# Reordering the head of a two-layer graph kernel: how many filter-spectrum steps stand between the head's rounds, and where a round's norm stands

## Chip, cores and metric

The kernel runs on one core of a Trainium2 chip. The metric is the device time of one execution in microseconds (us). The kernel before the change took 2195.82 us, the median of three runs between 2191.8 and 2198.84 us. The profile is of one execution, with a span of 2189.7 us.

## What is computed

The input is `x`, 128 graphs of 128 nodes with 256 features, and `adj`, one 128 x 128 adjacency matrix for each graph. Two layers follow each other, and each adds to `x` what it makes of the normalized `x`. Cut to what matters here:

```python
h = relu(layernorm(x))                                  # layer 0
xc = transpose(h)
c = relu(bn1(conv1d(xc, conv1_w)))                      # 1 tap
c = bn2(conv1d(c, conv2_w, pad=8))                      # 17 taps along the nodes
x_conv = transpose(relu(c + xc))
x_nmp = (exp(-dist(h)) * adj) @ relu(h @ w_msg.T + b_msg)
x = x + gru(concat(x_conv, x_nmp), h)
x = x + five_group_graph_conv(relu(layernorm(x)), adj)  # layer 1
```

All of it is in float32. The change is in the first fifth of the kernel: the norm, the one-tap convolution, and the preparation of the 17-tap convolution, which the kernel does in the frequency domain.

## The kernel before

The 128 graphs are worked on in blocks of four (`BB = 4`), 32 blocks in all. The first part of the kernel goes over them in two halves of 16 blocks (`HG = 64` graphs). For each half there is a head, which makes the spectra of the convolution's input, and a spectral stage, which multiplies them by the spectra of the filter taps, one frequency after the other. After both halves come the gates of layer 0 with layer 1 beside them; the change doesn't touch these.

**A head block** goes through five functions:

- `head_load` (line 189) brings 512 KB of `x` into a tile `ln`. There are three such buffers. The load goes through the SP queue, but for the very first.
- `head_norm` calls `layernorm`. For each of four graphs VectorE computes the statistics (lines 144 and 145), one instruction adds the epsilon (147), GpSimd raises it to the power -0.5 (149), and four VectorE instructions normalize in place (151). VectorE has to wait for GpSimd in between.
- `head_turn` transposes the block on TensorE (201) into two PSUM banks; ScalarE takes the relu into `ht` (202) and stores it for later, 512 KB through its own queue (203). From here the `ln` buffer is free for the load three blocks on.
- `head_conv1` is the one-tap convolution (215), again into two banks. VectorE adds the shift (218), and ScalarE takes the relu (219).
- `head_spectra` multiplies the result by a cosine and sine table (230) into four banks. VectorE copies two of them into the big tile `X` (236), ScalarE the other two (238).

**Tap spectra.** The spectra of the 17-tap filter are computed once, in eight tiles. `weight_spectra` is a generator: a tile takes four steps, and each step is 16 matmuls over four banks (172; a float32 matmul leaves two records in the profile, so a step is 32 records), which VectorE (178) and ScalarE (180) copy into a tile `sp` of 2560 KB, two banks each. There are two `sp` buffers. When a tile is complete it is stored into `vd` in DRAM through the SP queue (182), and the taps of the tile after the next are loaded, 1024 KB (162), also on the SP queue. The spectral stage reads `vd`, so it can't start before the last of these stores.

**How they are put together.** `some_spectra(k)` advances the generator by k steps. Six of the 32 steps are taken before the rounds of the first half; then `heads` runs one round for each block, and calls `between()` twice in a round. In the first half `between` is `some_spectra`, so two steps go with each round and the taps last for 13 rounds. In the second half `between` does nothing. Round i works on four blocks at once: the load of i + 3, the norm of i + 2, the transposition of i + 1, conv1 of i, and the spectra of i - 1. `heads_begin` fills this pipeline: it loads three blocks, normalizes two and turns the first; for the second half it is called two groups of frequencies before the end of the first spectral stage.

**What sets the order.** All PSUM tiles are handed out from one pool of eight banks in turn (`bank()`). The framework orders the instructions of each engine itself, when the kernel is built, and source order is the priority: something later in the source may move ahead of something earlier that is not ready by the framework's estimate. This can be seen in the profile, where the norm of one block is interleaved with the evictions of others on VectorE. Once built, that order is fixed.

Of the kernel before, what the change touches and what calls it, by code (L numbers as in the profile page):

```python
# [66 lines left out]
def gnn_kernel(ctx: ExitStack, tc: tile.TileContext, io, out: bass.AP):  # L67
# [16 lines left out]
    def bank():  # L84
        return psum.tile([P, 512], F32, tag="bank", name="bank")
# [21 lines left out]
    def constants():  # L107
        nc.sync.dma_start(vec, io["vec"])
        nc.sync.dma_start(wc1, io["wc1"].rearrange("(c p) o -> p c o", p=P))
        nc.sync.dma_start(fd, io["fd"])  # L110
        nc.sync.dma_start(idm, io["idm"])

        for j, v0 in enumerate((V_BN1, V_BN2)):
            g, b, m, v = (vec[:, v0 + 2 * q:v0 + 2 * q + 2] for q in range(4))
            sc, sh = bn[:, j, 0, :], bn[:, j, 1, :]
            ve = cst.tile([P, C], F32, name=f"bnve{j}")
            nc.vector.tensor_scalar(ve, v, EPS, None, op0=ALU.add)
            rs = cst.tile([P, C], F32, name=f"bnrs{j}")
            nc.gpsimd.tensor_tensor(rs, ve, mhalf[:, :C], op=ALU.pow)
            nc.vector.tensor_mul(sc, g, rs)  # L120
            nc.vector.tensor_mul(ve, m, sc)
            nc.vector.tensor_sub(sh, b, ve)

        bnb = hc.tile([P, 2 * C, P], F32, name="bnb")
        nc.vector.tensor_copy(bnb, bn[:, 0].rearrange("p q c -> p (q c)")[:, :, None].to_broadcast([P, 2 * C, P]))
        psb = bank()
        for q in range(2 * C):
            nc.tensor.matmul(psb[:, q * P:(q + 1) * P], bnb[:, q, :], ident, start=True, stop=True)
        nc.scalar.copy(bnr.rearrange("p q d -> p (q d)"), psb)
        nc.vector.tensor_mul(wc1, wc1, bnr[:, 0:1, :].to_broadcast([P, C, D]))  # L130
        nc.vector.tensor_add(brz, vec[:, V_IH:V_IH + 4], vec[:, V_HH:V_HH + 4])
# [28 lines left out]
    def taps_load(pool, c, q):  # L160
        w2 = pool.tile([P, WCH // 4, P], F32, tag="w2", name="w2", bufs=2)
        nc.sync.dma_start(w2, io["w2t"][:, c, q])
        return w2

    def weight_spectra(pool, c, q, w2):

        sp = pool.tile([P, LW, WCH], F32, tag="sp", name="sp", bufs=2)
        for t in range(WCH // 16):
            ps = [bank() for _ in range(4)]
            for j in range(4):  # L170
                for r in range(4):
                    nc.tensor.matmul(ps[r][:, j * LW:(j + 1) * LW], w2[32 * r:32 * r + KW, 4 * t + j, :],
                                     gt[32 * r:32 * r + KW, :], start=True, stop=True)
            for r in range(4):
                o0 = t * 16 + 4 * r
                dst, s = sp[:, :, o0:o0 + 4], ps[r][:, :4 * LW].rearrange("p (j d) -> p d j", j=4)
                if r % 2:
                    nc.vector.tensor_copy(dst, s)  # L178
                else:
                    nc.scalar.copy(dst, s)  # L180
            yield
        nc.sync.dma_start(vd[c, q], sp)
# [4 lines left out]
    def head_load(wk, i, queue):  # L187
        xs[i] = wk.tile([P, BB, D], F32, tag="ln", name="ln", bufs=3)
        queue.dma_start(xs[i], x[i * BB:(i + 1) * BB].rearrange("b n d -> n b d"))

    def head_norm(wk, i):
        layernorm(wk, xs[i], xs[i], P)

    def head_turn(wk, i):

        ln = xs.pop(i)
        ht = wk.tile([P, C, T], F32, tag="ht", name="ht", bufs=2)
        for c in range(C):
            ps = bank()
            for b in range(BB):  # L200
                nc.tensor.transpose(ps[:, b * N:(b + 1) * N], ln[:, b, c * P:(c + 1) * P], ident)
            nc.scalar.activation(ht[:, c, :], ps, AF.Relu)
        nc.scalar.dma_start(htd[i], ht)
        hcs[i] = ht

    def head_conv1(wk, i):
        ht = hcs.pop(i)
        h1 = wk.tile([P, BB, D], F32, tag="h1", name="h1", bufs=2)
        for h in range(BB // 2):
            ps = bank()  # L210
            pv = ps.rearrange("p (b d) -> p b d", b=2)
            for bb in range(2):
                b = 2 * h + bb
                for c in range(C):
                    nc.tensor.matmul(pv[:, bb, :], ht[:, c, b * N:(b + 1) * N], wc1[:, c, :],  # L215
                                     start=c == 0, stop=c == C - 1)
            hv = h1[:, 2 * h:2 * h + 2, :]
            nc.vector.tensor_tensor(hv, pv, sh1[:, None, :].to_broadcast([P, 2, D]), op=ALU.add)
            nc.scalar.activation(hv, hv, AF.Relu)
        h1s[i] = h1  # L220

    def head_spectra(X, i):
        h1 = h1s.pop(i)
        g0 = (i * BB) % HG
        for c in range(C):
            xv = X[:, c].rearrange("p a k (w g) -> p (a k) w g", w=2)
            for h in range(BB // 2):
                ps = bank()
                for bb in range(2):
                    nc.tensor.matmul(ps[:, bb * 2 * LW:(bb + 1) * 2 * LW], h1[:, 2 * h + bb, c * P:(c + 1) * P], fd,  # L230
                                     start=True, stop=True)
                s = ps[:, :4 * LW].rearrange("p (g w d) -> p d w g", g=2, w=2)
                dst = xv[:, :, :, g0 + 2 * h:g0 + 2 * h + 2]
                for w in range(2):
                    if h:
                        nc.vector.tensor_copy(dst[:, :, w], s[:, :, w])
                    else:
                        nc.scalar.copy(dst[:, :, w], s[:, :, w])
# [10 lines left out]
    def heads(wk, X, h, between):  # L249

        i0, i1 = h * NBH, (h + 1) * NBH
        for i in range(i0, i1 + 1):
            if i + 3 < i1:
                head_load(wk, i + 3, nc.sync)
            if i + 2 < i1:
                head_norm(wk, i + 2)
            if i + 1 < i1:
                head_turn(wk, i + 1)
            between()
            if i < i1:  # L260
                head_conv1(wk, i)
            between()
            if i > i0:
                head_spectra(X, i - 1)
# [60 lines left out]
    with front as es:  # L325
        xp = es.enter_context(tc.tile_pool(name="xp", bufs=1))
        hk = es.enter_context(tc.tile_pool(name="hk", bufs=1))
        X = xp.tile([P, C, NP_, 2, P], F32)
        with ExitStack() as ws:
            wp = ws.enter_context(tc.tile_pool(name="wp", bufs=1))  # L330
            todo = [(c, q) for c in range(C) for q in range(D // WCH)]
            head_load(hk, 0, nc.scalar)
            nc.sync.dma_start(gt, io["gt"])
            taps = [taps_load(wp, *todo[k]) for k in range(2)]
            head_norm(hk, 0)
            spectra = []

            def some_spectra(k=1):
                for _ in range(k):
                    if not spectra and todo:  # L340
                        spectra.append(weight_spectra(wp, *todo.pop(0), taps.pop(0)))
                    if spectra and next(spectra[0], STOP) is STOP:
                        spectra.pop(0)
                        if len(todo) > 1:
                            taps.append(taps_load(wp, *todo[1]))
                        some_spectra()

            some_spectra(3)
            constants()
            heads_begin(hk, 0)  # L350
            some_spectra(3)
            heads(hk, X, 0, some_spectra)
            while spectra or todo:
                some_spectra()
        bp = es.enter_context(tc.tile_pool(name="bp", bufs=1))
        nc.sync.dma_start(wms, io["wms"].rearrange("(c p) o -> p c o", p=P))
        nc.sync.dma_start(bms, row("bms", D + 3))
        nc.sync.dma_start(fw, row("fw", 5))
        nc.sync.dma_start(wih, io["wih"].rearrange("(c p) o -> p c o", p=P))
        nc.sync.dma_start(whh, io["whh"].rearrange("(c p) o -> p c o", p=P))  # L360
        for h in range(NH):
            if h:
                heads(hk, X, h, lambda: None)
            spectral(bp, X, h, lambda: heads_begin(hk, h + 1) if h + 1 < NH else None)
            if h == 0:
                gate_weights()

    wk = ctx.enter_context(tc.tile_pool(name="wk", bufs=1))
# [601 lines left out]
```

## Time and profile before

The profile's slices of time give each engine's busy time. The granted clock is a share of TensorE's full clock, and the DMA share is that of 16 DMA engines. Stages were told apart by the lines that run in them:

| stretch of the span | what runs | PE busy | DVE busy | clock | DMA share, GB/s |
|---|---|---|---|---|---|
| 20 to 40 us | head of half 0, first rounds | 17.84 of 20 | 13.47 | 0.66 | 0.85, 334 |
| 80 to 100 us | head of half 0, with tap spectra | 18.12 of 20 | 11.91 | 1.00 | 0.79, 289 |
| 120 to 140 us | the same | 18.15 of 20 | 11.93 | 0.83 | 0.76, 279 |
| 240 to 260 us | spectral stage of half 0 | 20.00 of 20 | 9.90 | 1.00 | 0.94, 312 |
| 380 to 400 us | head of half 1, no tap spectra | 20.00 of 20 | 16.34 | 1.00 | 0.45, 160 |

Over the whole span TensorE is busy for 2061.9 us (94%), VectorE for 1276.7 us (58%), ScalarE for 694.5 us and GpSimd for 580.5 us. PE is TensorE, DVE is VectorE, ACT is ScalarE, POOL is GpSimd, and SP is the engine that only issues DMAs. The first spectral matmul of half 0 starts at 205.91 us; that of half 1 at 431.56 us.

A busy time of TensorE has to be read with care: the ends of matmuls are modelled[...]. So the distance from the start of one group of matmuls to the next says more than the busy share.

### The profile page before, as it was taken

What the parts mean: (1) busy time and instruction counts of PE and PEld (TensorE: products, weight loads), DVE (VectorE), ACT (ScalarE), POOL (GpSimd) and SP (SyncE); (2) the same over time, 40 slices, a digit from 0 to 9 for tenths busy, and PEclk for the clock granted to TensorE, in tenths of its full rate; (3) what the DMA queues carried; (4) which work ended last, traced back from release to release, by engine and by line L of the source; (5) the groups of instructions that cost most, each with busy time, mean ns of one, the idle gap of its engine ahead of it and who ended that gap; (6) DMA issues with size and microseconds to landing.
All of it is one profiled execution on the core that took longest, in us unless ns stands there. A gap on an engine that the chain in (4) does not pass through costs nothing.

```text
span 2189.7 us, 31150 instructions
## 1 busy us (share of the span) xinstructions
PE 2061.9 (94%) x10981; PEld 1717.5 (78%) x10981; DVE 1276.7 (58%) x3518; ACT 694.5 (32%) x1424; POOL 580.5 (27%) x666
## 2 busy tenths in 40 slices
PE   7898988998999999999999999999999999999587
PEld 6777878987778778877888887788888778887576
DVE  6755447643555656665665666666566666655442
ACT  3442113411333333333333333333333333332222
POOL 3101531144222323322222332222233222212100
PEclk8998999999999999999999999999999999999787
DMA  8665984298412222221223222122322212221152
GB/s 335 252 242 184 300 273 172 94 298 256 143 52 73 70 62 72 72 71 52 71 87 109 83 71 72 51 72 88 110 83 72 71 51 71 92 81 53 55 151 84
DMA packets 200909, 260.11 MB, mean 119 GB/s; under 512 B 19378, under 2 KB 179378, under 8 KB 196146
## 3 DMA queue, kind: packets, MB, share of 16 engines
q1 hardware_dynamic: 192418, 219.85, 31.6%
q10 hardware_dynamic: 8336, 38.28, 4.7%
q8 instruction: 88, 1.44, 0.3%
q14 instruction: 67, 0.55, 0.1%
HBM read 175.63 MB, written 82.44 MB: 118 GB/s over the span
## 4 chain that ended last, share of the span: by engine, by line
PE 73%; DMA 8%; DVE 6%; POOL 3%; issue 1%; SPq 1%; ACT 0%; POOLq 0%; DVEq 0%; ACTq 0%
PE bank L550 29%; PE bank L299 5%; PE bank L586 5%; PE bank L773 5%; PE bank L790 5%; DMA hg<-xg 4%; PE bank L456 3%; PE bank L294 3%; PE bank L502 3%; PE bank L215 3%; PE bank L441 2%; PE bank L439 2%; PE bank L230 2%; DMA ln<-in_x_dram 1%; DMA w<-in_w_dram 1%; PE bank L617 1%
## 5 line engine op out<-in xcount | busy, mean ns | idle before, releaser
L550 PE MATMUL bank<-t,sw 128*128 128x256 f32 x1024 | 254.1, 381 | 1.1 <-DVE nn L565 1.1
L563 POOL TENSOR_TENSOR u<-u,m 128x256 f32<-128x256 f32 x96 | 73.1, 761 | 637.0 <-ACT m L561 613.0
L550 PEld LDWEIGHTS bank<-t,sw 128*128 128x128 f32 x1024 | 187.7, 191 | 24.6 <-DVE nn L565 1.2
L550 PE MATMUL bank<-t,wih 128*128 128x256 f32 x768 | 197.8, 380 | 0.0
L550 PEld LDWEIGHTS bank<-t,wih 128*128 128x128 f32 x768 | 146.2, 191 | 34.3 <-issue 10.7
L773 PE MATMUL bank<-ax,w 128*128 128x192 f32 (+12 forms) x592 | 129.4, 370 | 25.6 <-DMA w<-in_w_dram 22.7
L291 POOL TENSOR_TENSOR vs<-v 128x512 f32<-128x512 f32 x78 | 102.1, 1328 | 146.1 <-DMA v<-vd 81.1
L773 PEld LDWEIGHTS bank<-ax,w 128*128 128x128 f32 x592 | 104.4, 219 | 43.2 <-issue 29.7
L790 PE MATMUL bank<-w,hh 128*100 128x256 f32 (+8 forms) x552 | 133.3, 386 | 1.2 <-DMA w<-in_w_dram 1.2
L660 POOL TENSOR_TENSOR pw<-pw,mhalf 100x2 f32<-100x2 f32 (+7 forms) x69 | 50.3, 729 | 299.2 <-DVE pw L659 153.0
L456 PE MATMUL bank<-wms,ht 128*128 128x259 f32 x512 | 124.8, 387 | 5.1 <-DMA ht<-htd 5.1
L215 PE MATMUL bank<-wc,ht 128*128 128x256 f32 x512 | 127.2, 405 | 1.6 <-DVE sp L178 1.6
L586 PE MATMUL bank<-ht,whh 128*128 128x512 f32 x256 | 116.9, 600 | 0.0
L215 PEld LDWEIGHTS bank<-wc,ht 128*128 128x128 f32 x512 | 102.0, 205 | 17.4 <-DVE sp L178 1.8
L456 PEld LDWEIGHTS bank<-wms,ht 128*128 128x128 f32 x512 | 98.7, 193 | 20.8 <-issue 5.5
L550 PE MATMUL bank<-xc,wih 128*128 128x256 f32 x384 | 114.8, 381 | 0.0
L550 PE MATMUL bank<-xn,wih 128*128 128x256 f32 x384 | 114.7, 380 | 0.0
L790 PEld LDWEIGHTS bank<-w,hh 128*100 128x100 f32 (+8 forms) x552 | 92.2, 169 | 28.0 <-DMA w<-in_w_dram 1.4
L460 ACT ACTIVATE msg<-msg 128x512 f32<-128x512 f32 x64 | 40.3, 630 | 197.1 <-DVE msg L457 184.4
L289 DVE SCALAR_TENSOR_TENSOR s<-X 128x256 f32<-128x256 f32 x78 | 47.6, 613 | 94.2 <-PE bank L299 93.7
L149 POOL TENSOR_TENSOR rs<-ve,mhalf 128x4 f32<-128x4 f32 x32 | 32.3, 1008 | 232.9 <-DVE ve L147 232.9
L657 DVE BATCH_NORM_STATS2 st<-hg 100x6 f32<-100x256 f32 (+7 forms) x69 | 28.7, 419 | 108.8 <-DMA hg<-xg 108.7
(175 smaller groups left out, 4511.2 us busy)
## 6 DMA issues: line engine op xcount, KB each, us to landing
v<-vd SPq DMA_DIRECT2D x80, 512.0 KB
w<-in_w_dram SPq DMA_DIRECT2D x60, 512.0 KB
vd<-sp SPq DMA_DIRECT2D x8, 2560.0 KB
yd<-ys ACTq DMA_DIRECT2D x40, 512.0 KB
htd<-ht ACTq DMA_DIRECT2D x32, 512.0 KB
ht<-htd SPq DMA_DIRECT2D x32, 512.0 KB
ym<-yd SPq DMA_DIRECT2D x32, 512.0 KB
xt<-in_x_dram SPq DMA_DIRECT2D x32, 512.0 KB
```

The costliest lines, as they stand in the source:

```text
L215: nc.tensor.matmul(pv[:, bb, :], ht[:, c, b * N:(b + 1) * N], wc1[:, c, :], start=c == 0, stop=c == C - 1)
L291: nc.gpsimd.tensor_tensor(vs, vr, vi, op=ALU.add)
L294: nc.tensor.matmul(p1[:, :D], a[:, c], vs[:, c], start=c == 0, stop=c == C - 1)
L299: nc.tensor.matmul(ps[:, k * D:(k + 1) * D], u[:, c], w[:, c], start=c == 0, stop=c == C - 1)
L456: nc.tensor.matmul(ps[:, :D + 3], ht[:, c, b * N:(b + 1) * N], wms[:, c, :], start=c == 0, stop=c == C - 1)
L502: nc.tensor.matmul(ps[:, b * N:(b + 1) * N], msg[:, b, c * P:(c + 1) * P], e[:, b, :], start=True, stop=True)
L550: nc.tensor.matmul(ps, w, d, start=n == 0, stop=n == len(pairs) - 1)
L563: nc.gpsimd.tensor_tensor(got["u4"], got["u2"], got["m5"], op=ALU.add)
L586: nc.tensor.matmul(ps, whh[:, c, col:col + P], ht[:, c, :], start=c == 0, stop=c == C - 1)
L660: nc.gpsimd.tensor_tensor(pw[:n, 2:4], pw[:n, 0:2], mhalf[:n, 0:2], op=ALU.pow)
L773: nc.tensor.matmul(pv[:, q - q0, :], w1s[g][:, c, q * P:(q + 1) * P], ax[:, c, m0:m1], start=c == 0, stop=c == C - 1)
L790: nc.tensor.matmul(ps[:n, :D], hh[:, q, at:at + n], w2s[g][:, q, :], start=q == 0, stop=q == HID // P - 1)
```

## The change

The change has two parts, both in the head. Within a round of `heads`, conv1 of block i now comes first, then a call of `between`, then the transposition of block i + 1 and the norm of block i + 2, then the second `between`, then the spectra of block i - 1. Before, the norm came first, then the transposition, and conv1 stood between the two calls. This holds for both halves. And in the first half each `between` takes two steps of the tap spectra where it took one, so four steps go with a round, and the taps are through around block eight instead of around block thirteen.

It is meant to keep matmuls from standing behind a norm on VectorE's queue, and to have the taps' spectra stored early. No instruction is added or removed.

```diff
@@ heads @@
         for i in range(i0, i1 + 1):
             if i + 3 < i1:
                 head_load(wk, i + 3, nc.sync)
+            if i < i1:
+                head_conv1(wk, i)
+            between()
+            if i + 1 < i1:
+                head_turn(wk, i + 1)
             if i + 2 < i1:
                 head_norm(wk, i + 2)
-            if i + 1 < i1:
-                head_turn(wk, i + 1)
-            between()
-            if i < i1:
-                head_conv1(wk, i)
             between()
             if i > i0:
                 head_spectra(X, i - 1)
@@ with front as es @@
             heads_begin(hk, 0)
             some_spectra(3)
-            heads(hk, X, 0, some_spectra)
+            heads(hk, X, 0, lambda: some_spectra(2))
             while spectra or todo:
                 some_spectra()
```

## The prediction

> **What bounds the kernel now.** I read the 20 us slices first. From 206 us on nearly all of them have TensorE busy throughout at full clock; the change touches only the two heads (about 5 to 206 us and 320 to 432 us), so I asked for the stepped rounds of half 0 and for steady rounds of half 1 as two stretches. Columns: PE, PEld, DVE, ACT, POOL busy, clock, DMA share, GB/s.
> ```profile
> 28.85:179.00 150.15, 133.85 (x1305) 112.76 (x1306) 96.90 (x309) 56.81 (x149) 18.41 (x20) 0.92 0.67 246
> ...
> 345.00:410.00 65.00, 65.00 (x402) 60.87 (x401) 51.32 (x187) 28.38 (x77) 10.06 (x10) 1.00 0.43 155
> ```
> The reader should see that the half 1 rounds leave TensorE no gap, while the 13 stepped rounds of half 0 (150.15 / 13 = 11.55 us each) have 16 us of gaps, a clock of 0.92 and no engine that is full. The chain of waits in half 1 gives the undisturbed price of a round's pieces:
> ```profile
> 346.76 3.46 PE bank L215 x16
> 350.22 2.17 PE bank L230 x16
> 352.39 0.87 PE bank L201 x8
> ```
> So a plain round is 3.46 + 2.17 + 0.87 = 6.50 us of TensorE. A tap step is 1.06 us (32 records, from 94.34 to 95.40 us in the timeline). A stepped round before should take 6.50 + 2 x 1.06 = 8.62 us; it takes 11.55, a loss of 2.93 us a round. The timelines of TensorE, VectorE and SP around 160 us show how it is lost:
> ```profile
> 163.39 0.46 PE L172 MATMUL bank<-gt,w 17*128 17x80 f32 x6
> 166.83 1.96 PE L172 MATMUL bank<-gt,w 17*128 17x80 f32 x26 [2.98 <-DVE X L236]
> 168.72 6.10 PE L215 MATMUL bank<-wc,ht 128*128 128x256 f32 x16
> ```
> ```profile
> 165.47 0.76 DVE L144 BATCH_NORM_STATS2 st<-ln 128x6 f32<-128x256 f32 x2 [4.31 <-DMA ln<-in_x_dram]
> 166.14 0.54 DVE L236 COPY X<-bank 128x160 f32<-128x160 f32 x2
> ```
> ```profile
> 153.22 0.34 SPq L182 DMA_DIRECT2D vd<-sp  x1
> 153.66 10.20 SPq L189 DMA_DIRECT2D ln<-in_x_dram  x2
> ```
> Read backwards: conv1 ran at half clock (6.10 us for 16 records instead of 3.6). Ahead of it TensorE idled 2.98 us for a bank that VectorE's copies to X had to empty. They stood on VectorE behind the first statistics of a norm, which waited 4.31 us for its block of x. That block was issued at 153.66 us, just behind the 2560 KB store of a tap tile, and landed about 12 us later. In the stepped rounds VectorE waits so four times (10.0 us), and 13 times for GpSimd's power (14.3 us).
>
> [...] the busiest slice here, 180 to 200 us, has 354 GB/s at a share of 1.04[...].
>
> **The change part by part.**
>
> *Four steps a round.* Nothing is added: 26 steps stand in the rounds. They took 13 rounds at two; at four they take six rounds and a half. A four-step round needs 6.50 + 4 x 1.06 = 10.74 us of TensorE. VectorE, from the distances in its timeline: norm 3.0, wait for GpSimd 1.2, two shifts 1.2, eight tap copies at 0.41 = 3.3, four copies to X 1.0, in all 9.7 us. DMA: a tile's store and taps, a block of x and a block stored, by the page's sizes
> ```profile
> vd<-sp SPq DMA_DIRECT2D x8, 2560.0 KB
> ln<-in_x_dram SPq DMA_DIRECT2D x18, 512.0 KB
> ```
> are 2560 + 1024 + 512 + 512 KB = 4.72 MB[...]. If each round kept the loss of before, it would take 10.74 + 2.93 = 13.67 us[...]. [...] I take 14.2 us, with 13.2 and 16.5 as ends. The half round (two steps) takes 11.5. The other six of the old 13 rounds become plain, at 6.5 us as in half 1: 6 x 14.2 + 11.5 + 6 x 6.5 = 135.7 us against 150.15. **That is 14.5 us less.**
>
> *The stores are early.* They end near 125 us instead of 186.6, so the x loads of the last rounds and the first loads of vd no longer queue behind the last store. Before, the end of the head (191.1 to 205.9 us, 14.8 us for 3.46 + 2 x 2.17 = 7.8 us of TensorE) held VectorE waits for x of 2.8 and 0.5 us and TensorE idles of 3.0 and 0.8 us. Half 1's first norms still fall there; I count 3 us less. The spectral stage itself (PE busy 84.09 of 84.10 us) gains nothing.
>
> *conv1 first, the norm late (both halves).* The order adds no wait between instructions, but moves what stands behind a norm. Now the shifts of conv1 and the first tap copies have priority over it; behind it stand the second tap copies and the copies to X, hence spectra's banks. A norm takes 3.0 + 1.2 us on VectorE. Ahead of a blocked bank TensorE still has the transposition and two steps, 0.87 + 2.1 us, so up to 1.2 us a round may show, less than what a late block cost; it is inside the 2.93 us that I keep. In half 1 the start profits:
> ```profile
> 331.85 0.75 DVE L144 BATCH_NORM_STATS2 st<-ln 128x6 f32<-128x256 f32 x2 [6.43 <-DMA ln<-in_x_dram]
> ...
> 336.89 0.68 DVE L218 TENSOR_TENSOR h<-bank,bnr 128x512 f32<-128x512 f32 x1
> ```
> There a shift stands behind a norm that waits 6.43 us, and TensorE idles 6.43 us. With conv1 ahead, one more conv1 (3.5 us) can run in that wait; bounds 0 and 6, I take 3. The steady half 1 rounds are full on TensorE and stay at 6.5 us; VectorE there has only its 1.2 us wait for GpSimd to spare, so the new order could cost there: between 0 and 0.5 us in each of 13 rounds, I take 0.25, so 3 us, and another 1 us for the plain rounds of half 0.
>
> Sum: -14.5 - 3 - 3 + 3 + 1 = -16.5 us, so **2179 us**.
>
> **The rivals.**
>
> *DMA takes the place of the stalls, no change.* [...] For: [...] a store that waits for VectorE holds up the x loads behind it. Against: x loads have some two rounds until their norm. At 16.5 us a round: 99 + 11.5 + 39 = 149.5 us, a gain of 0.7 there; with 1 us from the end, 2194 us.
>
> *The new order stalls, slower.* A tile's first copy waits until the store two tiles back has landed, on VectorE and ScalarE ahead of all other evictions; before, a tile lasted 22.5 us and a store about 10, now they come within one round. If that wait and the cold clock after it bring the round to 18 us (108 + 11.5 + 39 = 158.5, +8.4), and half 1 pays 0.5 us in 13 rounds (+6.5) with 3 us back elsewhere, the time is 2207 us. For: a 2.98 us idle already cost a half clock.
>
> *All waits vanish.* Rounds [...] (79.2 + 10 + 39 = 128.2, -22), the end 6 and half 1's start 6 us shorter, no cost: 2162 us. For: each of these waits began at a late block. [...]
>
> **How the numbers follow.** Forecast 0.48, no change 0.19, slower 0.19, all waits vanish 0.14. The range reaches from the last case to near the slower one, 2160 to 2205 us. Faster by over 0.3% (below 2189.2 us) holds for the last case and nearly all of the first, and a little of the second: 0.64. Within 0.3%: 0.16. Slower (above 2202.4): 0.20.
>
> **What would show it right or wrong.** Right: seven rounds with tap matmuls of about 14 us, then plain ones near 6.5; the last vd store near 125 us; DMA share above 0.85 until then; the first spectral matmul near 190 us instead of 205.9; the head of half 1 no longer than before. Wrong: taps' copies that wait for a DMA, statistics that wait for x with evictions behind them as often as before, a granted clock below 0.9 up to 130 us, or half 1 rounds above 7 us.

## The result, and the profile after

The changed kernel takes 2182.4 us (median; 2179.8 to 2186.4), the one before 2195.9 us (2191.8 to 2198.8) beside it: a ratio of 0.9941, 95% interval 0.9919 to 0.9964, or 13.5 us less. The forecast was 2179 us. The time was met; the way to it was not, as the stages show. Executions of one and the same kernel differ by more than the change is worth (43 of the kernel before lie between 2186.3 and 2203.3 us), and each stage time below is from one profiled execution.

First the stages, in the view that gives busy time by stretch (columns: stretch, its length, busy time of PE, PEld, DVE, ACT and POOL with instructions, clock granted to TensorE, DMA share, GB/s): six four-step rounds; the plain rounds and the end of half 0; the head of half 1.

```profile
22.53:115.25 92.72, 81.61 (x994) 71.56 (x994) 60.20 (x168) 35.68 (x94) 16.99 (x18) 0.81 0.87 334
124.99:194.57 69.58, 64.98 (x368) 57.43 (x369) 51.25 (x181) 28.27 (x74) 13.17 (x12) 0.95 0.61 212
306.16:420.12 113.96, 106.49 (x634) 97.35 (x632) 75.32 (x251) 49.80 (x126) 14.60 (x14) 0.97 0.43 152
```

A four-step round takes 92.72 / 6 = 15.45 us, not 14.2. Its TensorE work is 10.74 us by the prediction's sum. TensorE is idle 92.72 - 81.61 = 11.1 us, 1.85 a round. The rest, (81.61 - 6 x 10.74) / 6 = 2.86 us, is time in which it works at half speed: the granted clock was 0.81, which the prediction had named as a sign against itself. So the loss of a round rose from 2.93 to 4.71 us.

One round in the timeline of TensorE (start, duration, engine and line; in brackets the idle before and who ended it):

```profile
84.58 3.62 PE L215 MATMUL bank<-wc,ht 128*128 128x256 f32 x16
88.13 2.03 PE L172 MATMUL bank<-gt,w 17*128 17x80 f32 x64
90.08 1.09 PE L201 MATMUL bank<-ident,ln 128*128 128x128 f32 x8
91.11 1.13 PE L172 MATMUL bank<-gt,w 17*128 17x80 f32 x32
92.60 1.52 PE L172 MATMUL bank<-gt,w 17*128 17x80 f32 x32 [0.37 <-DVE sp L178]
...
96.33 3.57 PE L230 MATMUL bank<-fd,h 128*128 128x160 f32 x12 [1.46 <-DVE sp L178]
99.69 4.57 PE L215 MATMUL bank<-wc,ht 128*128 128x256 f32 x16
```

The second bank of the spectra comes late, by 1.46 us, and then 12 records take 3.57 us (at full clock 12/16 of 2.17 us, so 1.63) and conv1 4.57 us instead of 3.46 (granted clock 0.50 over the 6.82 us from 94.78 us). But by the clock record, the trace's list of stretches at full and at half clock, this half clock began at 94.78 us, 0.1 us before that wait, so the late bank isn't what brought it. The 3.41 us ahead of it hold an idle of 0.37 us among tap steps (the columns of the stages again):

```profile
91.37:94.78 3.41, 3.04 (x68) 2.56 (x64) 2.19 (x11) 2.05 (x6) 1.01 (x1) 1.00 0.90 323
94.78:101.60 6.82, 5.36 (x18) 4.89 (x18) 3.80 (x12) 0.99 (x4) 0.00 (x0) 0.50 1.07 438
```

All six rounds have a half-clock phase. In four it began during the wait for that bank, in this one just before it, and in the first, which has no such wait, at 33.34 us behind idles of 0.16 us at most. On VectorE one sees what held the bank, here the same place of the round at 58 us:

```profile
61.62 0.76 DVE L144 BATCH_NORM_STATS2 st<-ln 128x6 f32<-128x256 f32 x2 [1.01 <-DMA ln<-in_x_dram]
...
64.71 0.74 DVE L151 TENSOR_SCALAR ln<-ln,mv,rs 128x256 f32<-128x256 f32 x2 [1.13 <-POOL rs L149]
65.36 0.88 DVE L178 COPY sp<-bank 128x320 f32<-128x320 f32 x2
```

The tap copies of the second pair of steps stand behind the norm and both its waits. In the waits of 20 to 190 us (in total, times, longest) the bank behind the norm is thus new, while the waits for x are shorter and more frequent than the four of before (10.0 us):

```profile
DVE st L144 <- DMA ln<-in_x_dram: 11.7, 10, 4.0
PE bank L230 <- DVE sp L178: 9.4, 5, 2.5
```

In half 1 one line answers to the one shown of before:

```profile
318.67 0.75 DVE L144 BATCH_NORM_STATS2 st<-ln 128x6 f32<-128x256 f32 x2 [8.16 <-DMA ln<-in_x_dram]
```

and TensorE still waits 6.41 us, until 324.95 us, for the relu of a transposed block that comes behind it. The head of half 1 takes 113.96 us, against 111.36 us before.

The difference can be added up from the starts of matmuls. "Start" is the first conv1, "rounds" from there to the conv1 of block 13, "end" from there to the first spectral matmul (us):

| kernel | start | rounds | end | first spectral matmul |
|---|---|---|---|---|
| before | 28.85 | 150.1 | 26.9 | 205.9 |
| after | 22.53 | 150.4 | 21.7 | 194.6 |
| new order, two steps | 22.3 | 156.4 | 21.1 | 199.8 |
| old order, four steps | 32.0 | 150.0 | 21.1 | 203.1 |

The last two rows are the first pair of experiments below, which split the change. A second profile of the changed half 0, from the run with tap-like matmuls in half 1, has 22.4, 153.4, 21.6 and 197.5 us: start and end repeat, the rounds only within 3 us.

The head of half 0 thus gains 6.3 us at its start and 5.2 us at its end, and nothing in the thirteen rounds. The cuts aren't quite even. A transposition and a tap step stood ahead of the first conv1 before and now come later, the step in the rounds and a transposition in the end. At full clock these are 0.87 + 1.06 = 1.93 us, so of the 6.3 us about 4.4 are saved (waits of 2.1 us, and half clock: 0.50 was granted from 22 to 28.85 us), the rounds gain 0.9 us and the end 6.1.

Of the rest, spectral stage 0 takes 111.6 instead of 114.3 us (-2.7), the head of half 1 +2.6, everything behind it +1.0; together -10.4 us of profile span (2179.3 against 2189.7). The -2.7 us are the tail of the old end: before, the stage began at half clock, and 5.21 us of it at 0.50 cost 2.6: from start to start 12 records took 5.24 us there, and behind it, at a clock of 1.00, 4 took 0.86 us, so that 12 would take 2.58.

```profile
205.91:211.12 5.21, 5.21 (x12) 4.13 (x13) 1.02 (x4) 0.57 (x1) 0.00 (x0) 0.50 0.00 0
```

### The profile page after: what moved, and what is told of

It is laid out like the page before. It is cut to its first block, busy times and chain, and to the rows that moved or that the text cites. A ratio compares the mean times of both kernels' runs of the same rounds, so it can differ in the third digit from the quotient of the medians.

```text
span 2179.3 us, 31120 instructions
## 1 busy us (share of the span) xinstructions
PE 2058.2 (94%) x10981; PEld 1716.7 (79%) x10981; DVE 1276.1 (59%) x3518; ACT 697.3 (32%) x1424; POOL 581.3 (27%) x666
## 4 chain that ended last, share of the span: by engine, by line
PE 75%; DMA 10%; DVE 8%; POOL 4%; issue 1%; SPq 1%; ACT 1%; POOLq 0%; DVEq 0%; ACTq 0%
PE bank L550 28%; PE bank L299 5%; PE bank L586 5%; PE bank L773 5%; PE bank L790 5%; PE bank L215 5%; DMA hg<-xg 4%; PE bank L456 4%; PE bank L230 3%; PE bank L294 3%; PE bank L502 3%; PE bank L441 2%; PE bank L439 2%; DMA ln<-in_x_dram 2%; PE bank L617 1%; DMA w<-in_w_dram 1%
## 5 line engine op out<-in xcount | busy, mean ns | idle before, releaser
L773 PE MATMUL bank<-ax,w 128*128 128x192 f32 (+12 forms) x592 | 131.2, 375 | 25.0 <-DMA w<-in_w_dram 22.4
L230 PE MATMUL bank<-fd,h 128*128 128x160 f32 x512 | 84.3, 321 | 10.4 <-DVE sp L178 9.4
```

What stands on the lines that cost most here:

```text
L773: nc.tensor.matmul(pv[:, q - q0, :], w1s[g][:, c, q * P:(q + 1) * P], ax[:, c, m0:m1], start=c == 0, stop=c == C - 1)
```

## The experiments

Three explanations of the 15.45 us stood first, by the names that the expectations use. DMA FLOOR: the rounds carry 0.87 of the DMA's share and can't be much shorter. BANKS: the late bank behind the norm costs its idle and lets the clock fall. BUFFERS: x comes late because there are only three buffers for it.

**New order, two steps a round.**

```diff
-            heads(hk, X, 0, lambda: some_spectra(2))
+            heads(hk, X, 0, some_spectra)
```

> The new order of a round, with the old two steps a round. Theory PACKING (the gain is that six stepped rounds become plain, the order by itself is worth little): 13 rounds of about 11.5 us as before, total 2191 to 2199 us. Theory ORDER (the gain is that conv1's evictions no longer stand behind a norm): rounds below 11 us, total about 2184 us.

Measured: 2194.7 us, ratio 0.9985 (0.9972 to 0.9997). The first spectral matmul comes 6.1 us earlier than before, but the head of half 1 takes 3.1 us longer (114.4 us), and spectral stage 0, which here waits 2.72 us just behind its first matmuls, 0.5 us.

**Old order, four steps a round.** This is the kernel before with one line changed, so the norm comes first, as it did.

```diff
-            heads(hk, X, 0, some_spectra)
+            heads(hk, X, 0, lambda: some_spectra(2))
```

> Four steps a round, with the old order (norm, transposition, steps, conv1, steps, spectra). Theory PACKING: most of the gain is here, first spectral matmul at 193 to 198 us, total 2182 to 2187 us. Theory ORDER: four steps behind a norm that comes first stall more than two did; no gain, 2195 us or more.

Measured: 2189.6 us, ratio 0.9977 (0.9965 to 0.9989); first spectral matmul 2.8 us earlier. Neither part alone gives the 0.9941. The order brings the early start (its first conv1 goes ahead of a transposition and a step that took 1.97 and 2.40 us before, at a granted clock of 0.50), and at two steps a round it pays for that with 6.3 us in the rounds. Four steps leave the rounds as they were, and the head of half 1 too (111.9 us). Either alone shortens the end by nearly 6 us, so this gain counts only once.

**Tap copies off VectorE.** All tap copies of the tile's first two steps go to ScalarE.

```diff
-                if r % 2:
+                if r % 2 and t >= 2:
```

> The changed kernel, with the tap copies of the two steps behind the norm all on ScalarE (VectorE keeps its half of the other two steps). Theory BANKS (four-step rounds take 15.4 us because spectra's second bank is emptied by a VectorE tap copy that stands behind the norm): that TensorE wait (five times 1.4 to 2.5 us) goes, rounds fall to 13.3 to 14 us, total about 2173 us. Theory DMA FLOOR (the rounds are set by 4.72 MB a round): rounds stay above 15 us, total within 3 us of the changed kernel, 2180 to 2185 us.

Measured: 2180.3 us, ratio 0.9938 (0.9915 to 0.9960): no better than the change. The wait at the spectra's bank is gone. In its place stand others (waits, 22 to 112 us):

```profile
DVE st L144 <- DMA ln<-in_x_dram: 19.1, 5, 7.0
PE bank L172 <- DVE sp L178: 8.3, 2, 6.1
ACT sp L180 <- DMA vd<-sp: 6.3, 2, 3.6
```

and the six rounds take 15.1 us on average, from 10.8 to 20.1. One of them (12.7 us) has no idle of TensorE that the timeline shows, so 15.4 is no floor; but it too has 3.4 us of half clock by the clock record. Another has neither. It takes 10.83 us, TensorE's own sum, at a clock of 1.00 and a DMA share of 0.94:

```profile
51.19:62.02 10.83, 10.82 (x170) 9.76 (x169) 7.01 (x21) 6.58 (x19) 1.74 (x3) 1.00 0.94 342
```

A single round is thus held neither by the DMA nor by its tap steps. The round behind it waits 6.13 us for a tap copy and takes 20.1.

**Loads of x on ScalarE's queue.**

```diff
-                head_load(wk, i + 3, nc.sync)
+                head_load(wk, i + 3, nc.scalar)
```

> The changed kernel, with the rounds' loads of x on ScalarE's DMA queue instead of SP's. Theory QUEUE (the blocks of x land late because they are issued and drained behind tap stores and vd loads): plain rounds of half 0 lose less than the 9 us they lose now, the 6.4 us wait at the start of half 1 shrinks, total 2172 to 2178 us. Theory BANDWIDTH (they are late because the DMA engines are full): no change, 2180 to 2185 us.

Measured: 2234.8 us, ratio 1.0179 (1.0153 to 1.0205), which no theory had. The issue of the load now has its place in ScalarE's own order, among copies and activations, as the stores of `ht` have in the changed kernel: there a relu ended at 61.41 us, the issue took 61.45 to 61.78 us, and the next tap copy began at 61.88 us. And x comes later than ever: VectorE's statistics wait 61.6 us in eight times, a four-step round takes some 24 us. That the loads wait behind ScalarE's work is the author's reading; the run's views don't show their issues. The run says nothing on the disputed cause, but something on queues: the loads did not come earlier on the queue that carries only the 512 KB of `ht` a round.

**A quarter of the store.** Only a quarter of each tap tile is stored, and the spectral stage reads that quarter again and again; three quarters of the tap spectra are left out. Once alone, once together with the tap copies on ScalarE.

```diff
-        nc.sync.dma_start(vd[c, q], sp)
+        nc.sync.dma_start(vd[c, q], sp[:, :LW // 4, :])
```

> The changed kernel, storing only a quarter of each tap tile (the first 20 of 80 columns) and reading that quarter again for every frequency; what is left out is three quarters of the tap spectra. A four-step round then moves 2.75 MB instead of 4.72. Theory DMA FLOOR: rounds fall from 15.4 to below 13.5 us, and granted clock over rounds rises. Theory BANKS (the stall at spectra's second bank, 1.4 to 2.5 us with a cold clock behind it, sets the round): rounds stay within 0.7 us of 15.4.

> The kernel with the tap copies behind the norm on ScalarE, also storing only a quarter of each tap tile (three quarters of the tap spectra are left out). If both DMA and banks bind, each alone hides the other: rounds of 11 to 12 us here, near TensorE's 10.7, where the copies alone gave 15.1. If DMA alone binds: the same as the quarter store by itself. If neither does: still about 15 us.

Measured: 2188.9 and 2198.6 us, one time each; four-step rounds of 12.3 to 22.6 and 15.4 to 19.7 us. For the first, 22 to 112 us:

```profile
22.00:112.00 90.00, 79.27 (x844) 70.08 (x841) 53.03 (x150) 30.49 (x79) 16.34 (x18) 0.74 0.55 185
```

The DMA share falls from 0.87 to 0.55, and the rounds get no shorter: DMA FLOOR, as the cause of 15.45 us, falls. But the runs don't isolate the rest. With the store shorter, VectorE's instructions come out in another order, the norm ahead of conv1's shifts, and so

```profile
92.18 0.75 DVE L144 BATCH_NORM_STATS2 st<-ln 128x6 f32<-128x256 f32 x2 [5.17 <-DMA ln<-in_x_dram]
```

holds the shift, hence a bank for 3.22 us; the clock (0.74) falls within that idle. The plain rounds behind are another matter: six of them take 42.0 and 41.8 us here, against 47.9 and 50.8 in the two profiles of the changed half 0.

**Three steps a round** (two, then one).

```diff
-            heads(hk, X, 0, lambda: some_spectra(2))
+            turn = [0]
+
+            def three():
+                turn[0] += 1
+                some_spectra(1 + turn[0] % 2)
+
+            heads(hk, X, 0, three)
```

> The new order with three steps a round (two in the first place, one in the second), so taps last 8.7 rounds and a round moves 3.8 MB [...] beside 9.7 us of TensorE. Theory DMA FLOOR: rounds of about 12.5 us; 8.7 of them and 4.3 plain ones against 6.5 and 6.5 are 8 us less than in the changed kernel, total about 2174 us. Theory BANKS: the loss a round stays near 4.7 us, rounds of 14.4 us; 8 us more than in the changed kernel, about 2190 us.

Measured: 2191.1 us, ratio 0.9977 (0.9963 to 0.9991). Rounds between 9.9 and 23.0 us; the first spectral matmul at 205.0 us.

**A fourth buffer for x** (room made by putting two start-up tensors into a tile that is free then).

```diff
-        xs[i] = wk.tile([P, BB, D], F32, tag="ln", name="ln", bufs=3)
+        xs[i] = wk.tile([P, BB, D], F32, tag="ln", name="ln", bufs=4)
```

> The changed kernel with four buffers for x instead of three (three small constants moved to make room), so a load no longer waits for a transposition. Theory BUFFERS (blocks of x land late in the first plain rounds and at the start of half 1 because their buffer comes free late): plain rounds of half 0 lose 2 to 4 us instead of 9, the 6.4 us wait at the start of half 1 goes, total 2168 to 2174 us. Theory BANDWIDTH (they are late because DMA is full): unchanged within 3 us, 2179 to 2186 us.

Measured: 2187.9 us, ratio 0.9968 (0.9947 to 0.9989). In the four-step rounds VectorE's statistics still wait four times for x, 5.7 us in all against 6.3, the bank stall of 1.46 us stays, and the rounds take 15.0 to 19.0 us. The six plain rounds take 47.1 us instead of 47.9, and half 1's start still waits 6.12 us. BUFFERS falls.

With these out of the way the half clock itself was in question. A half-clock phase occurred in nearly every four-step round, even in that round of the third experiment with 12.7 us and no visible idle. Hence a new theory, CLOCK: tap steps and transpositions, 5.1 us in one stretch, are themselves what lets the clock fall. The round of 10.83 us already speaks against it, and two runs tell it from BANKS.

**The stretch cut in two.** The spectra go between the first two steps and the transposition.

```diff
             between()
+            if i > i0:
+                head_spectra(X, i - 1)
             if i + 1 < i1:
                 head_turn(wk, i + 1)
             if i + 2 < i1:
                 head_norm(wk, i + 2)
             between()
-            if i > i0:
-                head_spectra(X, i - 1)
```

> The changed kernel with the pieces of a round in another order: conv1, two tap steps, the spectra of the block behind, the transposition of the next, the norm, two tap steps. Nothing is computed otherwise. CLOCK (the tap steps and the transposition, 5.1 us in one stretch, are themselves what lets the clock fall; spectra and the next conv1 then run at half clock): the stretches are now 2.1 and about 3.0 us with full matmuls between, so the granted clock of the four-step rounds rises from 0.81 to above 0.92, rounds fall from 15.4 to about 13.3 us, the first spectral matmul comes near 183 us, time about 2170 us. BANKS (an idle of 1.4 to 2.5 us of TensorE for a bank behind the norm is what lets it fall): the idle moves to another piece and the clock stays near 0.81, rounds 15 us or more, time 2180 to 2185 us. DMA [...]: rounds no shorter than 14.5 us, time 2175 us or more.

Measured: 2201.3 us, ratio 1.0033 (1.0017 to 1.0049), slower than before; granted clock 0.81 over 22 to 115 us, unchanged. The spectra run at full clock now, and the next conv1 takes the half clock, behind even a short idle:

```profile
90.84 2.44 PE L230 MATMUL bank<-fd,h 128*128 128x160 f32 x16
...
96.09 1.13 PE L172 MATMUL bank<-gt,w 17*128 17x80 f32 x30 [0.67 <-DVE X L236]
97.15 5.41 PE L215 MATMUL bank<-wc,ht 128*128 128x256 f32 x16
```

CLOCK's forecast is missed in each of its numbers.

**Tap-like matmuls in half 1.** Matmuls whose results nobody reads are added where half 0 has its steps: 32 of 17 rows per place in the first eight rounds, 16 of 128 rows in the later ones.

```diff
+        def fill():
+            k = 32 if calls[0] < 16 else 16
+            calls[0] += 1
+            ps = [bank() for _ in range(4)]
+            for m in range(k):
+                r, c, j = m % 4, m % 2, m // 4 % 4
+                rows = slice(32 * r, 32 * r + KW) if k == 32 else slice(0, P)
+                nc.tensor.matmul(ps[r][:, j * LW:(j + 1) * LW], wc1[rows, c, :P], gt[rows, :],
+                                 start=True, stop=True)
...
-                heads(hk, X, h, lambda: None)
+                heads(hk, X, h, fill)
```

> The changed kernel with matmuls added to the head of half 1, whose steady rounds (6.5 us, clock 1.0) have no tap steps, no copies of them and no store: into the two places of a round where half 0 has its steps, 32 matmuls of 17 rows each in the form of the tap steps (first eight rounds), or 16 matmuls of 128 rows each (the later rounds), about 2.1 us in either form; their results are read by nobody. CLOCK: without a stall and without DMA load the rounds with 17 rows lose their clock as half 0 does, granted clock about 0.8, 13 us a round instead of 10.7; the rounds with 128 rows stay at clock 1.0 and 10.7 us. BANKS or DMA: there is neither a late bank nor a load, so both kinds keep a clock of 1.0 and take 10.7 us. Kernel time 2182 plus 65 us (BANKS) or plus 80 to 85 us (CLOCK).

Measured: 2297.0 us, one time. Neither theory has it right, and that is the find. Rounds with 17-row matmuls alternate; here one with, one without a half clock, and one with 128 rows (stretches by busy time):

```profile
350.45:367.25 16.80, 15.84 (x171) 14.47 (x170) 7.94 (x30) 3.56 (x9) 2.01 (x2) 0.71 0.22 80
395.20:405.97 10.77, 10.77 (x171) 9.75 (x169) 3.54 (x10) 3.18 (x8) 0.00 (x0) 1.00 0.23 75
436.30:449.91 13.61, 13.61 (x106) 13.20 (x105) 5.78 (x20) 3.34 (x9) 1.01 (x1) 1.00 0.23 78
```

The same matmuls take 10.77 us without an idle, at clock 1.00, and 16.80 us where a bank comes 0.96 us late:

```profile
354.00 0.46 PE L370 MATMUL bank<-gt,wc 17*128 17x80 f32 x6
355.41 1.98 PE L370 MATMUL bank<-gt,wc 17*128 17x80 f32 x58 [0.96 <-DVE X L236]
357.32 1.92 PE L201 MATMUL bank<-ident,ln 128*128 128x128 f32 x8
359.17 3.72 PE L370 MATMUL bank<-gt,wc 17*128 17x80 f32 x64
```

The DMA share is 0.22 and 0.23, so the load of the DMA engines doesn't decide it. Against CLOCK: 17-row steps and transpositions without an idle kept the clock. (The 128-row matmuls take 3.69 us a place, not the 2.1 that the expectation assumed; their rounds of 13.61 us have TensorE full.) Against the forecast of BANKS: there was a late bank after all. In its mechanism BANKS stands here, in a sharper form: among tap steps an idle of 0.75 to 0.99 us (three of three: 0.96, 0.99 and 0.75 us) is followed by 10.2 us of half clock by the clock record, and the round is about 6 us longer, of which the idle itself is one. Rounds of 128 rows had no idle, so whether the same idle would cost the clock among full-row matmuls isn't tried. How short an idle suffices stays open as well: in the third experiment's round without a visible idle the second pair of steps took 2.57 instead of 2.03 us, so half a microsecond was lost in gaps too short for the timeline, and the clock fell. Nor does every such idle cost the clock. In the kernel before, one of 1.05 us within a transposition, with 0.56 us more among the tap step behind it, left it at 1.00, and so did idles of 0.97 us at 46 us and 1.05 us at 152 us:

```profile
81.41:88.24 6.83, 5.06 (x53) 4.01 (x52) 3.99 (x12) 3.56 (x11) 1.01 (x1) 1.00 0.81 335
```

A two-step round has one tap step (32 records, from 84.36 us here) between the transposition and conv1's matmuls of 128 rows, where the other has two steps in a row. Whether that is the reason isn't tested.

**Both edits at once**, tap copies on ScalarE and four buffers for x; and the same with x loaded four ahead, for half 1's start. (With four buffers the line numbers are 2 higher: L146 is L144.)

```diff
-                if r % 2:
+                if r % 2 and t >= 2:
...
-        xs[i] = wk.tile([P, BB, D], F32, tag="ln", name="ln", bufs=3)
+        xs[i] = wk.tile([P, BB, D], F32, tag="ln", name="ln", bufs=4)
```

> The changed kernel with two earlier single edits at once: the tap copies of the two steps ahead of spectra all on ScalarE, and a fourth buffer for blocks of x. Each alone took one of two idles away and gained nothing. IDLE (a short idle of TensorE, 0.5 us or more, among tap steps lets the clock fall [...]; without any idle the clock stays, as in the steady rounds with 17-row matmuls): with no late bank and no late x most rounds have no idle, granted clock of the four-step rounds above 0.9, rounds 13 to 13.5 us [...], first spectral matmul near 183 us, time about 2170 us. DMA or another wait in series (each idle that is taken away makes room for the next: copies on ScalarE that wait for a store): rounds 15 us or more, clock near 0.82, time 2178 to 2186 us.

and for the second of the pair, on top of that,

```diff
-        for k in range(1 if h == 0 else 0, 3):
+        for k in range(1 if h == 0 else 0, 4):
...
-            if i + 3 < i1:
-                head_load(wk, i + 3, nc.sync)
+            if i + 4 < i1:
+                head_load(wk, i + 4, nc.sync)
```

> The kernel of the run beside it, with blocks of x loaded four ahead instead of three, in both halves, so that the fourth buffer is used as soon as it is free. Half 0: as the run beside it, or a little later, since one more block of x goes ahead of a store. Half 1: if its start of 6.4 us of idle comes from the load of its fourth block, issued only once the first transposition has freed a buffer, the wait falls to under 1 us, with the half clock behind it, and the head of half 1 takes 107 us or less instead of 114; time 5 to 7 us under the run beside it. If the wait comes from the block's place behind the spectral loads in SP's order or from a slow DMA, it stays and the times are the same.

Measured: 2185.7 us, ratio 0.9948 (0.9933 to 0.9963), and 2182.4 us, ratio 0.9933 (0.9911 to 0.9955). The first forecast is missed: the rounds don't get free of idles. Clock 0.78 and 0.80 over 22 to 112 us; a round is 11.6 to 21.8 us in the first, with idles of 5.37, 4.52 and 2.42 us for shifts, copies to X and tap copies that VectorE gives late. Where one wait went, others came on the same engine. None of the kernels tried is measurably better than the changed one.

The second forecast is missed too, and the traces show what the wait hangs on. Four of these statistics belong to a norm. Counted from the start to 203 us, first in the changed kernel, then with one buffer more:

```profile
L144 DVE BATCH_NORM_STATS2 st<-ln x76: 389/408/429, 5.2 to 189.6; 128x6 f32<-128x256 f32 x76
```

```profile
L146 DVE BATCH_NORM_STATS2 st<-ln x80: 386/406/429, 5.1 to 191.1; 128x6 f32<-128x256 f32 x80
```

76 are 19 norms, blocks 0 to 18 (as in the kernel before), when in the program's text only 0 to 15 belong to this half; with four buffers it is 20. The framework, which sets each engine's order, thus pulled the norms forward as far as there were buffers. At the start of half 1 VectorE so comes upon the norm of a block whose buffer was freed by the transposition just done; its load was issued 1.07 us after that transposition began (309.61 to 310.68 us in the changed kernel), and conv1's shifts of an older block wait behind it. A fourth buffer only makes it a later block:

```profile
322.08 0.75 DVE L146 BATCH_NORM_STATS2 st<-ln 128x6 f32<-128x256 f32 x2 [9.93 <-DMA ln<-in_x_dram]
```

That the wait vanishes if the norm is held behind those shifts wasn't tried.

## Why the prediction was right, and where it was not

**Four steps a round, -14.5 us: wrong, +0.2 us.** This is the step that failed, and in three terms. The four-step round was put at 14.2 us and takes 15.45 (six of them: +7.5); the half round at 11.5 and takes 9.74 (-1.8); the six plain rounds at 6.5 and take 47.89 us, 7.98 each (+8.9). Together 150.35 us, against 135.7 forecast and 150.15 before. The first is the loss that was carried over unchanged from two-step rounds: "If each round kept the loss of before". A two-step round in the old order lost 2.93 us; here a round loses 4.71, of which 1.85 is idle and 2.86 half clock, and each of the six has a half-clock phase. That the time went there is measured. What lets the clock fall in these rounds is shown only in part: no run took both the idles and the half clock away. The third was not thought of. In the plain rounds

```profile
125.30 0.33 SPq L182 DMA_DIRECT2D vd<-sp  x1
125.72 4.24 SPq L189 DMA_DIRECT2D ln<-in_x_dram  x2
```

two blocks of x are issued just behind the last store, in the very rounds which then need a block every 6.5 us; three rounds take 8.7, 9.2 and 10.5 us, with an idle of 2.32 us ahead of the last one's conv1, which then ran at half clock (14 of its records took 6.03 us at 0.52, where 16 took 3.62 us at 1.00, from 131.56 us). The runs with a quarter of the store bear out that the store delays them: there the six plain rounds lose 2.8 to 3.0 us instead of 8.9.

**The DMA as floor: not shown.** That the DMA sets a lower bound for these rounds was the author's estimate. The share did come out at 0.87, as forecast, but with the store cut to a quarter the rounds were no shorter, and single rounds with the whole store took 10.83 and 12.7 us, under the 13.2 us of the forecast's lower end and under the 13.3 us that their 4.72 MB would take at the 354 GB/s of the busiest slice before (an estimate). Six rounds on end never came below 15.0 us on average with four steps, at shares of 0.86 to 0.91. Whether the DMA would hold them near 13 to 14 us (these times multiplied by the share, an estimate) is open. Nor are those 354 GB/s a ceiling for what a trace counts: 438 GB/s passed between 94.78 and 101.60 us, and 411 between 20 and 30 us before.

**The end, -3 us: right in kind, -5.2 us.** The waits of 3.0 and 0.8 us named there are gone. But the new order with the old pace of stores gained as much (21.1 us), so the end doesn't need the early stores that the prediction gave as the reason; the order alone is enough. And that the spectral stage "gains nothing" was read from busy time, 84.09 of 84.10 us, which doesn't show a half clock: its first 5.21 us ran at 0.50, and without the idles ahead of it the stage is 2.7 us shorter.

**The order.** "Up to 1.2 us a round" for the bank behind the norm had the right place, the spectra, but was too small: 1.4 to 2.5 us, in five of the six rounds, and the half clock on top. The plain rounds' 1 us is part of the 8.9. Half 1's steady rounds, +3 us, stayed at 6.50 us: 0. Half 1's start, -3 us, came out as a head longer by 2.6 us: the wait moved to the norm of another block, and a new one of 1.06 us came, since the second conv1 now follows directly on the transposition that it reads. So "The order adds no wait between instructions" was wrong there; the order alone costs 3.1 us in this head, four steps alone 0.5. The gain of the order lies where the prediction had none, at the start: the first conv1 is at 22.53 us instead of 28.85, of which some 4.4 us are saved and not only moved.

The sum was -16.5 us; the two profiles differ by -10.4 us and the medians by -13.5. From the forecast to the profiles' difference: +13.7 in the rounds (+0.2 instead of -14.5 + 1), -6.3 at the start and -2.2 at the end, +2.6 in half 1's head (forecast -3 + 3), -2.7 in spectral stage 0 and +1.0 behind, in which no step saw a change; together +6.1. The 3.1 us between profiles and medians come from which execution was profiled: that of before was the fastest of its four (2191.8 us). The forecast's number was right by compensation, that is by luck, and its marks told so. The last store at 125.30 us and the share of 0.87 came true. But the four-step rounds took more than 14 us, the plain ones 7.98 instead of 6.5, the first spectral matmul came at 194.6 us and not near 190, and the head of half 1 grew. Two of the signs of being wrong came too: a granted clock below 0.9, and statistics that wait for x more often than before.

## What to carry to other kernels

An idle has no fixed price: among small matmuls one of 0.96 us came with a round six longer in one run (16.80 against 10.77 us), with 10.2 us of half clock behind it, and in the kernel before one of 1.05 us left the clock at 1.00. So a loss taken over from another arrangement needs its own look at the clock in the new one. Here VectorE, in an order that is fixed when the kernel is built, serves both a norm, which waits for a load, and the copies that free banks: taking one wait away moved the loss to the next (idles of 5.37, 4.52 and 2.42 us with both edits at once), and one more buffer only let the norm run further ahead (20 norms up to 203 us instead of 19). And a change whose total is as forecast should still be split by stage: here the stage that was to bring all brought nothing.

## What the runs showed of the hardware

- **The clock fell behind less than a microsecond of idle, and not each time.** In the run with tap-like matmuls in half 1, idles of 0.96, 0.99 and 0.75 us among 17-row matmuls and transpositions were followed by 10.2 us of half clock, three of three times, while the same matmuls without an idle kept a clock of 1.00; a round took 16.80 against 10.77 us. In the changed kernel 0.37 us came before a fall, at 94.78 us; in the kernel before 0.97 to 1.05 us, three times, did not bring one. So in these runs the length of an idle alone doesn't decide.
- **Here matmuls of 17 rows came 3.6 times as fast as those of 128.** 64 records of 17-row matmuls of 80 columns, which the program puts in turn on rows from 0, 32, 64 and 96, took 2.03 us (the changed kernel, 88.13 us), 32 records of 128-row ones of the same width 3.69 us (the run with tap-like matmuls): 32 against 115 ns each. What makes the difference wasn't tested.
- **A DMA's issue has its place in its engine's order.** In the changed kernel the issue of a store on ScalarE's queue took 61.45 to 61.78 us, between a relu that ended at 61.41 and a tap copy that began at 61.88 us. The loads of x moved to that queue made the kernel 39 us slower than before; VectorE's statistics waited 61.6 us for x.
